# The tail of an eight-layer megakernel by pairs of sequences: last feed-forward layer, cross attention and second local stack in another order

## The chip, the core and the metric

The kernel runs on one core of a Trainium2 chip. The time is microseconds on the device for one launch; the profile is one execution taken by the hardware profiler. Five engines run side by side, each with its own instruction stream in a fixed order: TensorE (PE, with its weight loads shown apart as PEld), VectorE (DVE), ScalarE (ACT), GpSimd (POOL) and SyncE (SP, which here only issues DMAs). They wait for each other through semaphores.

## What is computed

The input `x` is eight sequences (B = 8) of 128 rows by 128 features; a context of 8 x 77 rows of 128 features stands beside it. Four blocks of layers follow each other, each of a cross attention and a feed-forward part. The change touches the end only, from the last of six layers of `L2_ffn` on. Cut to what matters, in float32:

```python
# L2_ffn: 6 layers, 16 heads of 64, window 32;  L3_ffn: 2 layers, 8 heads of 64, window 64
for i in range(DEPTH):
    x = attn_layer(shift_tokens(x), Wqkv[i], q_scale[i], k_scale[i], Wo[i]) + x
    x = ffn_layer(shift_tokens(x), ln_g[i], ln_b[i], W1[i], b1[i], W2[i], b2[i]) + x
# attn_layer: q, k normalised per head and rotated, softmax over a local window, times v, times Wo
# ffn_layer:  layer norm, a * gelu(gate) with 341 hidden features, times W2
x = x + L2_ffn(x)                                    # six layers inside, then the outer sum
x = x + L3_xattn(layernorm(x), context)              # 8 heads of 64 over 77 context rows
x = x + L3_ffn(layernorm(x))                         # two layers inside
```

Each sequence is independent of the others in these parts: sequence b of a layer needs only sequence b of the layer before. So the order in which sequences and layers are worked is free.

## The kernel before

All work is first recorded as steps in a plan, and then emitted. `Plan.add` takes the engines on which a step may run with an estimated duration, the values that it reads and writes and the buffers that it opens. The number of a step in this recording is its rank. `Plan.arranged` then runs a list scheduler over the steps: at each moment a free engine takes the ready step of lowest rank that is at most 600 ranks (for SP any number, unless `within` says otherwise) beyond the first step not yet started, and for whose buffers there is room. So the order of the calls in `plan_later` sets ranks, the scheduler sets the order on each engine, and this order is then fixed in the program. Buffers are shared by everything in this part: 48 of 128x512 floats ("big"), 8 banks of PSUM ("mm"), two rooms for attention weights ("w") and two for the rest of a layer's weights ("wr"). A step far ahead of the first unstarted one must leave a quarter of a kind free.

The pieces that the change orders, with their lines:

- `Local.first` (L1850) of one sequence and layer: `shifted` (L1900) transposes the sequences of a group, `projected` (L1911) makes queries and keys (matmuls of L1914), `queries_keys` (L1918) squares (L1935), rotates (L1936, L1938), sums (L1940) and adds (L1941) them, `inv_root` (L1960) makes the inverse norms, L1954 scales. `Blocks.turned` (L1785) then transposes through DRAM: DVE transposes blocks (L1793), SP writes them out (L1794) and reads them back (L1795).
- `Local.rest` (L1859) of one sequence: values, `weighed` (scores L2023, exponentials L2030), sums and outputs (`by_quarters` L2084, L2090 in L2_ffn, `by_halves` L2063, L2069 in L3_ffn), division (L2038 to L2052), projection (L1998) and the sum into `y` (L2002).
- `Local.gated` (L2099) of a group of sequences: shift (by DMA, L2114, in L2_ffn; by a matmul, L2120, in L3_ffn), layer norm, gates (L2145), gelu (L2152) with its loads of ACT's tables, L2159, L2161, down matmuls (L2169), and the sum into `y` or, at the last layer, `x` (L2174).
- `Local.end` (L1863) adds `y` to `x` (L1866, POOL); `Local.begin` (L1845) makes the layer norm of `x` for a group and starts a stack.
- `plan_xattn_64` (L1678): cross attention of four sequences (`half`): norm, one transposing step (L784), four query projections of 128x512 (L791), then `attend_64` (scores L970, softmax L834 to L853, outputs L981, projection L992) for one sequence after the other, and the sum into `x` (L1771). It yields between these pieces. Its keys and values were computed ahead of time and put into DRAM; `Kept.get` (L1759) loads them (L1761). An earlier block uses the same function with `kept=None`.
- `plan_later` (L2225): `order` is the list in which `first` and `rest` of all sequences are to be called. `some(n)` calls `first` for sequences a little ahead (two beyond the current one, in the second stack one), and then `rest` for the next. `along` steps through a cross attention between such calls.

Below, pair p is sequences 2p and 2p+1. In the tail the calls stand so: last layer of L2_ffn for pairs 0 and 1; `end` for both; cross attention of sequences 0 to 3 stepped through beside the last layer of pairs 2 and 3; `begin` of L3_ffn for sequences 0 to 3; `end` for 4 to 7; the second L3_ffn layer's weights; cross attention of sequences 4 to 7 beside the first L3_ffn layer of pairs 0 and 1; `begin` for 4 to 7; first layer of pair 2, attention of pair 0 in the second layer, first layer of pair 3, attention of pair 1; `gated` of the second layer for sequences 0 to 3 at once, and their store; then pairs 2 and 3.

Of the kernel before, what the change touches and what calls it, by code (L numbers as in the profile page):

```python
# [19 lines left out]
ALU = mybir.AluOpType  # L20
# [4 lines left out]
P = 128  # L25
B = 8
KC = 77
EPS = 1e-5
# [194 lines left out]
class Chip:  # L223
# [40 lines left out]
    def get(self, pack, name, lo=0, n=None):  # L264
        o, size = self.at[pack][name]
        return self.packs[pack][:, o + lo : o + (size if n is None else lo + n)]
# [56 lines left out]
def spread(ap, n, at):  # L323

    ap = ap.unsqueeze(at)
    shape = list(ap.shape)
    shape[at] = n
    return ap.to_broadcast(shape)
# [208 lines left out]
class Plan:  # L537
# [24 lines left out]
    def part(self, whole, get):  # L562

        return Val(None, lambda _: get(whole()), whole)
# [706 lines left out]
class Routed:  # L1271
# [251 lines left out]
    def behind(self, b, load):  # L1523

        self.w.c.tc.add_manual_dep(load.ins, self.got[b].name, mybir.DependencyInfo(
            mybir.DependencyClass.Sync, mybir.DependencyReason.DATA), reason="not in the way of these rows")
# [18 lines left out]
class Context:  # L1545
# [34 lines left out]
    def keys(self, h):  # L1580
        w = self.w
        c, nc = w.c, w.c.nc
        kT, kb, heads = w.tile([P, 4, KC]), self.kbs[h], c.get("cst", "heads4")
        self.rotated(kT, lambda: c.ctxT[:, h * 4 * KC : (h + 1) * 4 * KC], [], "k", 1, 4, KC)
        w.plan.add({"POOL": 2300}, lambda e: nc.gpsimd.tensor_tensor(
            kb().rearrange("p b i k -> p i b k"), spread(kT(), 4, 1), heads.unsqueeze(2).unsqueeze(3).to_broadcast([P, 4, 4, KC]),
            ALU.mult), [kT], [kb, *self.was[0]])
# [5 lines left out]
    def values(self, b):  # L1593
        c = self.w.c
        self.w.values_8(b, c.get("w", "L2_Wv"), c.get("row", "L2_xattn_bv"), self.vzs[b % 4])
# [82 lines left out]
def plan_xattn_64(w, nch, wq, wkv, wo, gamma, beta, bias, finish, kept=None):  # L1678


    c, nc, plan, inner = w.c, w.c.nc, w.plan, nch * P

    def half(h):
        xs = w.xs[4 * h : 4 * h + 4]
        xn, xT = w.tile([P, 4, P]), w.tile([P, 4, P])
        w.normed(lambda k: xn()[:, k, :], lambda k: xs[k](), xs, [xn], 1.0 + EPS, EPS * EPS)
        tp = w.turn(lambda k: xn()[:, k, :], [xn], opens=[xT])
        plan.add({"DVE": 683}, lambda e: nc.vector.tensor_scalar(xT(), tp(), gamma, beta, ALU.mult, ALU.add), [tp], [xT])
        for g in range(nch // 4):
            yield from group(h, g, xT)  # L1690

    def keys(h, k):
        ps, kT = w.bank([P, 4, KC]), w.tile([P, 4, KC])
        w.mm(lambda: ps().rearrange("p b k -> p (b k)"), lambda: wkv[:, k * P : (k + 1) * P],
             lambda: c.ctxT[:, h * 4 * KC : (h + 1) * 4 * KC], [], [ps], 520, opens=[kT])
        w.copy(kT, ps, [ps], [kT], 430, 470)
        return kT

    def values(b, g):
        ps, v = w.bank([KC, 512]), w.tile([KC, 512])  # L1700
        w.mm(ps, lambda: c.ctxT[:, b * KC : (b + 1) * KC], lambda: wkv[:, inner + g * 512 : inner + (g + 1) * 512], [], [ps],
             860, opens=[v])
        w.copy(v, ps, [ps], [v], 591, 682)
        return v

    def ahead():

        return [v for h in range(2) for v in (*(keys(h, k) for k in range(nch)), *(values(4 * h + j, 0) for j in range(4)))]

    def group(h, g, xT):  # L1710
        qTs = []
        if kept is None:
            kTs, v_of = [keys(h, k) for k in range(4 * g, 4 * g + 4)], lambda b: values(b, g)
        else:
            kTs = [kept.get([P, 4, KC], 8 * h + k) for k in range(4)]
            v_of = lambda b: kept.get([KC, 512], 8 * h + 4 + b % 4)
        for k in range(4 * g, 4 * g + 4):
            ps, qT = w.bank([P, 4 * P]), w.tile([P, 4 * P])
            w.mm(ps, lambda k=k: wq[:, k * P : (k + 1) * P], lambda: xT().rearrange("p b s -> p (b s)"), [xT], [ps], 860,
                 opens=[qT])  # L1720

            def part(e, qT=qT, ps=ps):
                if e == "ACT":
                    nc.scalar.mul(qT(), ps(), 0.125)
                else:
                    nc.vector.tensor_scalar(qT(), ps(), 0.125, None, ALU.mult)

            plan.add({"ACT": 597, "DVE": 683}, part, [ps], [qT])
            qTs.append(qT)
        yield  # L1730
        for j in range(4):
            b = 4 * h + j
            finish(b, w.attend_64(qTs, j * P, kTs, j, v_of(b), wo[:, 4 * g : 4 * g + 4, :],
                                  bias if g == 0 else None))
            if j < 3:
                yield

    return (half, ahead, kept) if kept else half


class Kept:
# [14 lines left out]
    def flat(t):  # L1756
        return t if len(t.shape) == 2 else t.rearrange("p b k -> p (b k)")

    def get(self, shape, i):  # L1759
        v = self.w.tile(shape)  # L1760
        self.w.plan.add({"SP": 500}, lambda e: self.w.c.nc.sync.dma_start(  # L1761
            self.flat(v()), self.rooms[i][: shape[0], 0 : int(np.prod(shape[1:]))]), [self.there[i]], [v], within=300)
        return v


# [456 lines left out]
    w.ys = [w.plan.fixed(w.y[:, b, :]) for b in range(B)]  # L2222


def plan_later(w, route, l2x, l2, l3x, l3, stored):  # L2225


    order = [(l2, l, b) for l in range(6) for b in range(B)]
    order += [(l3, l, b + j) for l, b in ((0, 0), (0, 2), (0, 4), (1, 0), (0, 6), (1, 2), (1, 4), (1, 6)) for j in range(2)]
    given = set()  # L2230
    at = {"first": 0, "rest": 0}

    def some(n):

        for i in range(n):
            while at["first"] < min(at["rest"] + 1 + (2 if at["rest"] < 48 else 1), len(order)) and order[at["first"]] in given:
                loc, l, b = order[at["first"]]
                loc.first(l, b)
                at["first"] += 1
            loc, l, b = order[at["rest"]]  # L2240
            loc.rest(l, b)
            at["rest"] += 1
            if i < n - 1:
                yield

    def side_by_side(*parts):
        for _ in zip_longest(*parts):
            pass

    def each(one, bs):  # L2250
        for b in bs:
            one(b)
            yield

    def begin(loc, b0, n):
        loc.begin(b0, n)
        given.update((loc, 0, b0 + k) for k in range(n))

    def gated(loc, l, b0, n=4):
        loc.gated(l, b0, n)  # L2260
        given.update((loc, l + 1, b0 + k) for k in range(n))

    def last(b0, n):
        l3.gated(1, b0, n, True)
        stored(b0, n)

    (one, layer), (l3x, ahead, kept) = l2x, l3x
    ahead = ahead()
    for k in range(4):
        side_by_side(each(one, (2 * k, 2 * k + 1)))  # L2270
        if k == 0:

            behind = lambda transfer: route.behind(1, transfer)
            kept.put(ahead, [w.xs[1]], behind)
            l2.layers[0] = l2.weights(0, [w.xs[1]], behind)
            w.plan.add({"SP": 5000}, lambda e: behind(w.c.load("w3")), [w.xs[1]], [])
        layer(2 * k, 2)
        begin(l2, 2 * k, 2)
    def along(steps, *counts):
        for n in counts:  # L2280
            side_by_side(some(1))
            for _ in range(n):
                next(steps, None)

    def pairs(loc, l, b0, n):
        for b in range(b0, b0 + n, 2):
            side_by_side(some(2))
            gated(loc, l, b, 2)

    side_by_side(some(4))  # L2290
    plan_flag(w)
    gated(l2, 0, 0, 2)
    gated(l2, 0, 2, 2)
    pairs(l2, 0, 4, 4)
    for l in range(1, 5):
        pairs(l2, l, 0, B)
    pairs(l2, 5, 0, 4)
    l2.end(0, 4)
    steps = l3x(0)
    along(steps, 0, 1)  # L2300
    gated(l2, 5, 4, 2)
    along(steps, 1, 1)
    gated(l2, 5, 6, 2)
    for _ in steps:
        pass
    begin(l3, 0, 4)
    l2.end(4, 4)
    l3.layers[1] = l3.weights(1)
    steps = l3x(1)
    for b in (0, 2):  # L2310
        along(steps, 1, 1)
        gated(l3, 0, b, 2)
    for _ in steps:
        pass
    begin(l3, 4, 4)
    for b in (4, 6):
        pairs(l3, 0, b, 2)
        side_by_side(some(2))
    last(0, 4)
    for b in (4, 6):  # L2320
        side_by_side(some(2))
        last(b, 2)


def store(c, out, b0, n):
# [83 lines left out]
```

## Time and profile before

| what | us |
|---|---|
| median of 3 runs (lowest, highest) | 1453.41 (1450.79, 1457.18) |
| the profiled execution, whole | 1462.85 |
| its span, first to last instruction | 1461.1 |
| TensorE busy in the span | 1343.9 |
| DVE, ACT, POOL busy in the span | 1111.7, 841.5, 837.9 |
| the stretch 1190 to 1461.1: TensorE busy | 228.7 of 271.1 |
| the same stretch: DVE, ACT, POOL busy | 185.5, 144.5, 125.2 |

Lines of the profile name the engine, the source line and the operation, then output tile <- input tiles, partitions x elements, and how many. A bracket at the end of a row of the timeline gives the idle time before it and what ended that. "PEclk" is the clock that TensorE was granted, as a share of full speed. One float32 matmul shows as two instructions, so "x6" of L2145 is three matmuls.

The last layer of L2_ffn runs from about 1120 to 1245 us, the cross attention of L3 between about 1190 and 1300, and L3_ffn from 1235 to the end. In the layers before (600 to 1100 us) TensorE is busy 475.9 of 500 us and DVE 466.2.

### The profile page before, as it was taken

The page shows a single profiled execution, that of the slowest core. Times are in us where ns is not written, and L with a number is a line of the kernel's source. Part 1 is how long each engine was busy: PE and PEld are TensorE (multiplying, and loading weights), DVE is VectorE, ACT ScalarE, POOL GpSimd, SP SyncE. Part 2 cuts the span into 40 slices and gives each one's busy share as a digit, 9 for nine tenths or more (in the row PEclk, how much of TensorE's full clock was granted, in tenths as well). Part 3 has the DMA queues.
Part 4 walks back from the last instruction along what each step waited for, and adds up shares of the span by engine and source line. Part 5 has one row for each costly group of instructions (what it writes and reads, how often), then busy time and mean ns, then how long its engine had stood idle before and what let it go on. Part 6 is the DMA issues. An engine that isn't in the chain of part 4 may idle for free. (4 is left out here: it accounts for less than half of the span.)

```text
span 1461.1 us, 39652 instructions
## 1 busy us (share of the span) xinstructions
PE 1343.9 (92%) x15451; PEld 949.1 (65%) x15451; DVE 1111.7 (76%) x2344; ACT 841.5 (58%) x1752; POOL 837.9 (57%) x1343
## 2 busy tenths in 40 slices
PE   8999999898888899999999999999899997798986
PEld 7777777665675566566666766766566766474655
DVE  7543676423478998998999989998889965869772
ACT  4565565243435457566666666766556754565653
POOL 4210236310577886876778767786768842738461
PEclk9999999999999999999999999999999999899998
DMA  9401001489421456455446545654654561304230
GB/s 309 167 1 44 2 2 59 132 300 354 141 70 37 138 182 209 154 176 193 151 143 223 180 127 170 201 165 150 218 165 125 160 216 50 117 1 145 88 109 25
DMA packets 217612, 204.40 MB, mean 140 GB/s; under 512 B 31646, under 2 KB 166366, under 8 KB 216264
## 3 DMA queue, kind: packets, MB, share of 16 engines
q1 hardware_dynamic: 211528, 196.54, 41.2%
q0 software_dynamic: 1536, 3.15, 0.7%
q8 instruction: 123, 2.02, 0.6%
q10 hardware_dynamic: 4352, 2.10, 0.5%
q14 instruction: 73, 0.60, 0.1%
HBM read 129.49 MB, written 70.68 MB: 137 GB/s over the span
## 5 line engine op out<-in xcount | busy, mean ns | idle before, releaser
L1941 POOL TENSOR_TENSOR big<-big,big 128x512 f32<-128x512 f32 x224 | 284.8, 1279 | 106.2 <-DVE big L1938 76.8
L1914 PE MATMUL mm<-wide,big 128*128 128x512 f32 x672 | 310.3, 603 | 6.3 <-DVE big L773 3.0
L771 ACT COPY big<-mm 128x512 f32<-128x512 f32 (+6 forms) x289 | 147.2, 519 | 162.3 <-PE mm L784 48.2
L1954 POOL TENSOR_TENSOR big<-big,few 128x512 f32<-128x512 f32 x224 | 227.3, 1045 | 1.9
L1935 ACT ACTIVATE big<-mm 128x512 f32<-128x512 f32 x224 | 132.4, 596 | 152.6 <-PE mm L1914 150.1
L1793 DVE STREAM_TRANSPOSE big<-big 128x512 f32<-128x512 f32 (+1 forms) x248 | 209.9, 867 | 10.8 <-POOL big L1954 10.2
L1914 PEld LDWEIGHTS mm<-wide,big 128*128 128x128 f32 x672 | 121.9, 192 | 133.4 <-issue 110.1
L1936 DVE TENSOR_TENSOR big<-mm,big 128x512 f32<-128x512 f32 x224 | 154.7, 691 | 15.1 <-ACT big L1935 13.4
L1938 DVE TENSOR_TENSOR big<-mm,big 128x512 f32<-128x512 f32 x224 | 153.9, 687 | 0.7 <-ACT big L1935 0.7
L1940 DVE TENSOR_REDUCE few<-big 128x8 f32<-128x512 f32 x224 | 152.4, 680 | 0.7 <-ACT big L1935 0.7
L2030 ACT ACTIVATE big<-mm 128x512 f32<-128x512 f32 x224 | 120.6, 600 | 50.7 <-PE mm L2023 48.2
L2023 PE MATMUL mm<-big,big 64*64 64x96 f32 (+2 forms) x3584 | 127.4, 275 | 7.2 <-DMA big<-blocks 4.7
L1998 PEld LDWEIGHTS mm<-narrow,big 128*128 128x128 f32 x896 | 108.5, 194 | 37.0 <-DVE big L2052 19.3
L2023 PEld LDWEIGHTS mm<-big,big 64*64 64x64 f32 x3584 | 125.8, 207 | 9.8 <-issue 5.6
L1998 PE MATMUL mm<-narrow,big 128*128 128x128 f32 x896 | 116.8, 282 | 16.5 <-DVE big L2052 8.9
L2090 PEld LDWEIGHTS mm<-big,big 128*32 128x32 f32 x3072 | 86.9, 110 | 28.1 <-issue 26.6
L784 PE MATMUL mm<-ident,big 128*128 128x128 f32 (+1 forms) x486 | 73.0, 284 | 33.0 <-ACT big L823 11.7
L2090 PE MATMUL mm<-big,big 128*32 128x128 f32 x3072 | 93.8, 273 | 0.0
L784 PEld LDWEIGHTS mm<-ident,big 128*128 128x128 f32 (+1 forms) x486 | 54.7, 144 | 59.4 <-ACT big L823 15.5
L773 DVE COPY big<-mm 77x512 f32<-77x512 f32 (+6 forms) x93 | 56.7, 624 | 46.3 <-PE mm L784 18.6
L2052 DVE SCALAR_TENSOR_TENSOR big<-mm,big 128x512 f32<-128x512 f32 x112 | 73.6, 684 | 2.0 <-PE mm L2090 0.3
L1495 DVE TENSOR_TENSOR big<-mm,p_col 128x512 f32<-128x512 f32 x32 | 20.7, 687 | 66.4 <-PE mm L784 55.6
(288 smaller groups left out, 2506.3 us busy)
## 6 DMA issues: line engine op xcount, KB each, us to landing
blocks<-big SPq DMA_DIRECT2D x224, 256.0 KB, 2.1
big<-blocks SPq DMA_DIRECT2D x224, 256.0 KB, 3.2
big<-in_experts_dram SPq DMA_DIRECT2D x128, 256.0 KB, 4.9
wide<-in_l2a_dram SPq DMA_DIRECT2D x6, 1536.0 KB
narrow<-in_l2b_dram SPq DMA_DIRECT2D x6, 534.0 KB, 10.9
narrow<-in_l2o_dram SPq DMA_DIRECT2D x6, 512.0 KB
blocks<-big SPq DMA_DIRECT2D x24, 128.0 KB, 1.9
big<-blocks SPq DMA_DIRECT2D x24, 128.0 KB, 3.4
```

Source lines behind the costliest of these rows:

```text
L771: nc.scalar.copy(out(), in_())
L1793: plan.add({"DVE": 150 + 138 * n}, lambda e: nc.vector.transpose(*within(u(), t())), [t], [u])
L1914: self.plan.add({"PE": 892}, lambda e: nc.tensor.matmul(ps(), lhsT=hs()[:, j, :], rhs=wqkv()[:, o : o + 512], start=True, stop=True), [hs, ...
L1935: yield lambda e: nc.scalar.activation(sq(), heads(), AF.Square)
L1936: yield lambda e: nc.vector.tensor_tensor(t1(), heads(), spread(rot()[:, 2 * kind, :], 8, 1), ALU.mult)
L1938: yield lambda e: nc.vector.tensor_tensor(halves(t2()), halves(heads())[:, :, ::-1, :], sin(), ALU.mult)
L1940: yield lambda e: nc.vector.tensor_reduce(ss()[:, lo : lo + 8], sq(), AX.X, ALU.add)
L1941: yield lambda e: nc.gpsimd.tensor_tensor(t1(), t1(), t2(), ALU.add)
L1954: plan.add({"POOL": 1062}, lambda e, t=t, t1=t1, i=i: nc.gpsimd.tensor_tensor(t().rearrange("p (c g d) -> p g c d", c=4, g=8), t1().rearra ...
L1998: nc.tensor.matmul(out(), lhsT=oT()[:, k, :], rhs=wo()[:, 4 * g + k, :], start=(g == 0 and k == 0), stop=(4 * g + k == nch - 1))
L2023: nc.tensor.matmul(sc[s]()[at : at + 64, k, q:end], lhsT=kT()[lo : lo + 64, k, at : at + 64], rhs=of_q(k, lo, q, end), start=False, stop=( ...
L2090: nc.tensor.matmul(avs[half]()[32 * t : 32 * t + 32, k, :], lhsT=vs[t // 2]()[:, at : at + 32], rhs=prs[t]()[:, k, :], start=True, stop=True)
```

## The change

The cross attention is made for any run of sequences (`part(b0, n)`) instead of halves, and the kept keys are loaded for two sequences (columns `b0 % 4 * KC` on of the kept tile, 154 of 308), so 16 loads of keys instead of 8. The estimates handed to the planner become formulas in n that give nearly the same numbers for n = 4. `LAST` writes out the order by pairs: A is the last layer of L2_ffn, X the cross attention, C and D the two layers of L3_ffn. Cross attentions that were begun are stepped through beside the following pieces, one step of each at a time; before C of a pair its cross attention is run to its end, and `begin` follows for the pair. `end` follows each A. The second layer's weights are no longer asked for early, but where that layer's first `first` stands. The look-ahead of `some` in L3_ffn goes from one sequence to two. D is done by pairs throughout, so its `gated` and the stores too: four of each instead of three.

```diff
@@ plan_xattn_64 @@
+    def part(b0, n, *parts):
+        xs = w.xs[b0 : b0 + n]
+        xn, xT = w.tile([P, n, P]), w.tile([P, n, P])
+        w.normed(lambda k: xn()[:, k, :], lambda k: xs[k](), xs, [xn], 1.0 + EPS, EPS * EPS, n=n)
+        tp = w.turn(lambda k: xn()[:, k, :], [xn], opens=[xT], n=n)
...
+        for at, m in parts or ((0, n),):
+            for g in range(nch // 4):
+                yield from group(b0 + at, m, g, lambda at=at, m=m: xT()[:, at : at + m, :], xT)
+
     def half(h):
...
+        return part(4 * h, 4)
...
-            kTs = [kept.get([P, 4, KC], 8 * h + k) for k in range(4)]
+            h = b0 // 4
+            kTs = [kept.get([P, n, KC], 8 * h + k, b0 % 4 * KC) for k in range(4)]
...
-            ps, qT = w.bank([P, 4 * P]), w.tile([P, 4 * P])
+            ps, qT = w.bank([P, n * P]), w.tile([P, n * P])
@@ plan_later @@
+LAST = "A0 A1 X0 A2 X1 A3 C0 X2 X3 C1 C2 C3 D0 D1 D2 D3".split()
...
-    order = [(l2, l, b) for l in range(6) for b in range(B)]
-    order += [(l3, l, b + j) for l, b in ((0, 0), (0, 2), (0, 4), (1, 0), (0, 6), (1, 2), (1, 4), (1, 6)) for j in range(2)]
+    order = [(l2, l, b) for l in range(5) for b in range(B)]
+    order += [({"A": l2, "C": l3, "D": l3}[k], {"A": 5, "C": 0, "D": 1}[k], 2 * int(p) + j) for k, p in LAST if k != "X" for j in range(2)]
...
-            while at["first"] < min(at["rest"] + 1 + (2 if at["rest"] < 48 else 1), len(order)) and order[at["first"]] in given:
+            while at["first"] < min(at["rest"] + 1 + (2 if at["rest"] < 48 else 2), len(order)) and order[at["first"]] in given:
...
-    pairs(l2, 5, 0, 4)
-    l2.end(0, 4)
-    steps = l3x(0)
-    along(steps, 0, 1)
-    gated(l2, 5, 4, 2)
-    along(steps, 1, 1)
-    gated(l2, 5, 6, 2)
-    for _ in steps:
-        pass
-    begin(l3, 0, 4)
-    l2.end(4, 4)
-    l3.layers[1] = l3.weights(1)
-    steps = l3x(1)
-    for b in (0, 2):
-        along(steps, 1, 1)
-        gated(l3, 0, b, 2)
-    for _ in steps:
-        pass
-    begin(l3, 4, 4)
-    for b in (4, 6):
-        pairs(l3, 0, b, 2)
-        side_by_side(some(2))
-    last(0, 4)
-    for b in (4, 6):
-        side_by_side(some(2))
-        last(b, 2)
+    attending = []
+
+    def along(steps):
+        for _ in steps:
+            for ahead in attending:
+                next(ahead, None)
+
+    for k, p in LAST:
+        b = 2 * int(p)
+        if k == "X":
+            attending.append(l3x(b, 2))
+            continue
+        if k == "C":
+            for _ in attending[0]:
+                pass
+            attending.pop(0)
+            begin(l3, b, 2)
+        along(some(2))
+        next_of = {"A": lambda: gated(l2, 5, b, 2), "C": lambda: gated(l3, 0, b, 2), "D": lambda: last(b, 2)}
+        next_of[k]()
+        if k == "A":
+            l2.end(b, 2)
```

On the engines, the programs are alike up to some place between 1120 and 1160 us of the profile before. After that TensorE's order puts pair 0's cross attention among the last L2_ffn layer of pairs 2 and 3, the projections of pair 0's first L3_ffn layer before the last feed-forward of pair 3, the cross attention of pairs 2 and 3 among the first L3_ffn layer of pairs 0 and 1, and all first layers ahead of nearly all second layers. From the scores of sequence 6 in the second layer on, the order is the same in both.

More of the change, by code (lines that the diff above doesn't have):

```diff
@@ L1681, in plan_xattn_64, with keys @@
     c, nc, plan, inner = w.c, w.c.nc, w.plan, nch * P
-    def half(h):
[L1684 to L1693, printed above, removed]
+    def part(b0, n, *parts):
[3 more added lines that the diff above has]
+        tp = w.turn(lambda k: xn()[:, k, :], [xn], opens=[xT], n=n)
+        plan.add({"DVE": 145 + 134 * n}, lambda e: nc.vector.tensor_scalar(xT(), tp(), gamma, beta, ALU.mult, ALU.add), [tp], [xT])
+        for at, m in parts or ((0, n),):
+            for g in range(nch // 4):
+                yield from group(b0 + at, m, g, lambda at=at, m=m: xT()[:, at : at + m, :], xT)
+    def half(h):
+        return part(4 * h, 4)
+    def keys(b0, n, k):
+        ps, kT = w.bank([P, n, KC]), w.tile([P, n, KC])
         w.mm(lambda: ps().rearrange("p b k -> p (b k)"), lambda: wkv[:, k * P : (k + 1) * P],
-             lambda: c.ctxT[:, h * 4 * KC : (h + 1) * 4 * KC], [], [ps], 520, opens=[kT])
-        w.copy(kT, ps, [ps], [kT], 430, 470)
+             lambda: c.ctxT[:, b0 * KC : (b0 + n) * KC], [], [ps], 130 * n, opens=[kT])
+        w.copy(kT, ps, [ps], [kT], 130 + 75 * n, 150 + 80 * n)
         return kT
@@ L1706, in ahead, with group, scale @@
     def ahead():
-        return [v for h in range(2) for v in (*(keys(h, k) for k in range(nch)), *(values(4 * h + j, 0) for j in range(4)))]
-    def group(h, g, xT):
+        return [v for h in range(2) for v in (*(keys(4 * h, 4, k) for k in range(nch)), *(values(4 * h + j, 0) for j in range(4)))]
+    def group(b0, n, g, of_x, xT):
         qTs = []
         if kept is None:
-            kTs, v_of = [keys(h, k) for k in range(4 * g, 4 * g + 4)], lambda b: values(b, g)
+            kTs, v_of = [keys(b0, n, k) for k in range(4 * g, 4 * g + 4)], lambda b: values(b, g)
         else:
-            kTs = [kept.get([P, 4, KC], 8 * h + k) for k in range(4)]
+            h = b0 // 4
+            kTs = [kept.get([P, n, KC], 8 * h + k, b0 % 4 * KC) for k in range(4)]
             v_of = lambda b: kept.get([KC, 512], 8 * h + 4 + b % 4)
         for k in range(4 * g, 4 * g + 4):
-            ps, qT = w.bank([P, 4 * P]), w.tile([P, 4 * P])
-            w.mm(ps, lambda k=k: wq[:, k * P : (k + 1) * P], lambda: xT().rearrange("p b s -> p (b s)"), [xT], [ps], 860,
+            ps, qT = w.bank([P, n * P]), w.tile([P, n * P])
+            w.mm(ps, lambda k=k: wq[:, k * P : (k + 1) * P], lambda: of_x().rearrange("p b s -> p (b s)"), [xT], [ps], 215 * n,
                  opens=[qT])
-            def part(e, qT=qT, ps=ps):
+            def scale(e, qT=qT, ps=ps):
                 if e == "ACT":
@@ L1726, in part @@
                     nc.vector.tensor_scalar(qT(), ps(), 0.125, None, ALU.mult)
-            plan.add({"ACT": 597, "DVE": 683}, part, [ps], [qT])
+            plan.add({"ACT": 180 + 104 * n, "DVE": 145 + 134 * n}, scale, [ps], [qT])
             qTs.append(qT)
         yield
-        for j in range(4):
-            b = 4 * h + j
+        for j in range(n):
+            b = b0 + j
             finish(b, w.attend_64(qTs, j * P, kTs, j, v_of(b), wo[:, 4 * g : 4 * g + 4, :],
                                   bias if g == 0 else None))
-            if j < 3:
+            if j < n - 1:
                 yield
-    return (half, ahead, kept) if kept else half
+    return (part, ahead, kept) if kept else half
 class Kept:
@@ L1757, in flat, with get @@
         return t if len(t.shape) == 2 else t.rearrange("p b k -> p (b k)")
-    def get(self, shape, i):
+    def get(self, shape, i, lo=0):
         v = self.w.tile(shape)
         self.w.plan.add({"SP": 500}, lambda e: self.w.c.nc.sync.dma_start(
-            self.flat(v()), self.rooms[i][: shape[0], 0 : int(np.prod(shape[1:]))]), [self.there[i]], [v], within=300)
+            self.flat(v()), self.rooms[i][: shape[0], lo : lo + int(np.prod(shape[1:]))]), [self.there[i]], [v], within=300)
         return v
@@ L2278, in plan_later @@
         begin(l2, 2 * k, 2)
[L2279 to L2283, printed above, removed]
     def pairs(loc, l, b0, n):
```

## The prediction

> **What bounds the kernel now.** I read the page's parts 1 and 2 first, then busy time by stretch over the tail, then TensorE's own instructions in order of time.
>
> ```profile
> span 1461.1 us, 39652 instructions
> PE 1343.9 (92%) x15451; PEld 949.1 (65%) x15451; DVE 1111.7 (76%) x2344; ACT 841.5 (58%) x1752; POOL 837.9 (57%) x1343
> ...
> PE   8999999898888899999999999999899997798986
> ...
> PEclk9999999999999999999999999999999999899998
> ```
>
> TensorE is busy 92% of the span, and its weak slices lie at the end, in the part that the change reorders. Stretches of that part (columns: busy us and count for PE, PEld, DVE, ACT, POOL; then granted clock, DMA share, GB/s):
>
> ```profile
> 1190.00:1226.00 36.00, 32.81 (x489) 26.21 (x478) 24.44 (x64) 20.15 (x56) 8.59 (x18) 1.00 0.34 115
> 1226.00:1266.00 40.00, 27.57 (x110) 15.10 (x110) 25.09 (x52) 17.58 (x36) 24.48 (x40) 0.79 0.26 84
> 1266.00:1306.00 40.00, 38.70 (x517) 30.83 (x514) 30.79 (x82) 26.65 (x68) 10.77 (x21) 1.00 0.17 55
> 1306.00:1350.00 44.00, 35.73 (x259) 20.85 (x257) 38.19 (x63) 25.68 (x55) 36.52 (x63) 0.92 0.36 115
> 1350.00:1388.00 38.00, 36.39 (x364) 24.37 (x362) 28.83 (x57) 23.08 (x47) 17.36 (x32) 1.00 0.28 90
> 1388.00:1424.00 36.00, 31.53 (x212) 19.49 (x216) 27.17 (x50) 20.36 (x39) 22.86 (x39) 0.91 0.34 110
> 1424.00:1461.10 37.10, 26.00 (x193) 19.91 (x192) 11.01 (x28) 11.04 (x21) 4.59 (x12) 0.81 0.09 24
> ```
>
> Full stretches alternate with weak ones. In the weak ones before the end the clock falls too, so idle time is paid twice:
>
> ```profile
> 1212.30 1.46 PE L2145 MATMUL mm<-big,narrow 128*128 128x256 f32 x6
> ...
> 1230.49 2.93 PE L2145 MATMUL mm<-big,narrow 128*128 128x256 f32 x6 [3.90 <-ACT big L2135]
> ...
> 1241.75 7.89 PE L1914 MATMUL mm<-wide,big 128*128 128x512 f32 x18
> 1256.69 1.63 PE L784 MATMUL mm<-ident,big 128*128 128x128 f32 x4 [7.05 <-ACT big L823]
> ```
>
> The same six gate matmuls (L2145) take 1.46 us warm and 2.93 us after the gap. From such rows, idle plus excess over the warm row, five stalls come out:
> - A, 1226 to 1238: idle 3.90 + 1.48, excess 1.47 + 1.15 (L2145, L2159): 8.0. The feed-forward of pair 3 in layer 5, then the norm of all four sequences 0 to 3, have nothing beside them.
> - B, 1250 to 1265: idle 7.05, excess 0.97 + 0.81 + 1.13 (L784, L2023, L791): 10.0. Four sequences' projections are issued, and the next cross attention waits for all of pairs 2 and 3.
> - C, 1307 to 1318: idle 1.37 + 0.54 + 0.64 + 1.48, excess 1.84: 5.9. The four-wide norm of sequences 4 to 7.
> - D, 1328 to 1348: idle 4.2, excess 1.8: 6.0. Scores wait for their block transposes.
> - E, 1388 to 1402: idle 4.1, excess 2.55: 6.6. Pair 3's first layer is late.
>
> Sum 36.5 us. The end from 1424 is a chain (scores, attention, shift, norm, gates, down, store).
>
> **The change, part by part.** *What is computed per sequence stays.* The eight 128x512 query matmuls become sixteen 128x256: TensorE time the same (L1914's 0.43 per instruction against L2145's 0.22). Their evictions: ACT's 128x256 copy is 354 ns against 598 for 128x512, so 16 x 0.354 - 8 x 0.598 = +0.9 us, on ACT and DVE, which were busy 144.5 and 185.5 of these 271 us. The roots of four-wide norms (POOL 0.19 + 1.03 + 0.25 + 0.20 = 1.67) become two two-wide ones (0.19 + 0.75 + 0.24 + 0.20 = 1.38): five of them, +5.4 us of POOL, busy 125 of 271. These lie beside TensorE: 0. Uncovered they would cost the 6.3.
>
> *The last feed-forward in pairs* adds a switch of ACT's tables. Row: L2154 loads take 1283 ns, with 0.1 us idle before six of them. The Trainium skill, "ScalarE: Activation LUTs", section "What ACT_TABLE_LOAD costs", speaks against it: about 1.28 us for the load plus 1.38 us of drain per switch. Two more loads: 2.6 us by the row, 5.3 by the page. I take the row, and nothing on the path, since pairs 0 and 1 of the last layer are followed by other sequences' work; uncovered 2.6.
>
> *Kept keys by pairs.* 16 key loads of 77 KB for 8 of 154 KB, values as before: 24 loads for 16.
>
> ```profile
> L1761 SPq DMA_DIRECT2D big<-kept x16: 297/424/522, 1155.0 to 1236.7; - x16
> ...
> DMA to landing us min/median/max: 4.6/5.0/5.4
> ```
>
> Eight issues more are 8 x 0.42 = 3.4 us of SP, in order with the block transfers (L1794, L1795). In the new order eleven kept loads stand among those of the last layer's sequences 3 to 7, and five between the transposed output and input of pair 3's gate; 5 x 0.42 = 2.1, against the 1.8 us which SP waited there for the output to land. Waits on a freed buffer are new there; behind such a load stand block inputs, and scores wait for these. SP's worst wait at L1761 was 0.5 us. Bounds: 0 and 8 x 0.5 + 3.4 = 7.4; I take 1.5, near the row.
>
> *The order* is the point. Durations below are sums of warm rows standing between two TensorE steps in the changed order ("cover"), against the chain outside TensorE.
> - A: pair 0's norm now follows cross attention of sequence 1. Chain: add 0.30, statistics 0.6, root 1.4 with gaps 0.3, scaling 0.9, handovers 1: 4.5; cover 2.5 (a transposing step 0.5, scores 0.65, pair 2's down matmuls 1.35): 2.0 left. Pair 3's gate chain took 18.2 us (last L1998 end 1212.3 to L2145 at 1230.5), cover 16 with the 2.0: 2.2 left. With clock about 5.0; saved 3.0.
> - B: projections to scores took 20.9 us for the first of four sequences (1237.74 to 1258.68); without the queue of four, rows add to 18.2 (projection 0.86, squares and reductions 4.9, root 2.7, scale 2.0, transposes 1.7, out 2.1, in 3.2, issues 0.8). Cover in the new order: four projections and two values 5.2, pair 3's gates and down 4.0, cross attention of sequences 2 and 3 4.6, queries and scores of the next 3.2: 17. Left 1.2 to 3.9; I take 2.5, with clock 4.0; saved 6.0.
> - C: the norms of pairs 1, 2, 3 have covers 4.5, 10 and 3.2 against 4.5: 1.3 left, and 1.3 from transpose to gates of pair 1: 2.6; saved 3.3.
> - D: covers of the first scores of pairs 1 and 2 are 18.2 and 18.3, left 0 to 2.8 each: 2.8 together; saved 3.2.
> - E: pair 3's first layer now stands ahead of the whole last layer; its shift has 6.4 of cover against 3.9 for shift to transpose (1442.72 to 1446.60), and the last layer's scores have 21 to 36. Left 0.6; saved 6.0.
> - The end: from the scores of sequence 6 on, TensorE's order is the same in both. Saved 0.
>
> Saved 21.5, less 1.5 for SP: **20 us**. Against the profiled execution, 1462.85, that gives 1443; the median of the runs shown is 1453.41, 9.4 lower, and the same subtraction gives **1433**. What is late next is DVE: work issued to it in the tail is nearly that of TensorE.
>
> The other rule: the Trainium skill, "TensorE: Matmul & The Clock Gate", "Part 1: The HAM clock gate (the "warmup" mystery)", has the clock halved after an idle window of about 3.4 us. Rows: C's gaps of 1.37, 0.54 and 0.64 in 2.6 us halved it as well (L2145 2.45, clock 0.83), and E's did. By the rule only A and B carry an excess, and the saving loses up to the 1.84 + 1.8 + 2.55 in C to E, 6.2: 14 us. I take the rows.
>
> **Rivals.**
> 1. *All five stalls go*: 1453.4 - 36.5 = 1417. For it: covers exceed those of before nearly everywhere. Against: A and B keep chains that are longer than their cover.
> 2. *The stalls move*: DVE sets the pace. For it: DVE ran 38.19 of 44 us from 1306 to 1350; cross attention's reductions now fall among the projections' DVE work. Against: 27 and 31 in the two full stretches. If A to D save a third of their 15.5 (5.2), E half of its 6.0 (3.0), and SP costs 4.0: gain 4.2, 1449.
> 3. *Slower: the pulled-forward cross attention starves the last layer.* From 1150 to 1190 TensorE has almost no slack (busy 38.95 of 40 us), and 48 big buffers are shared; two cross attentions in flight hold up to twenty (four keys, four queries, inputs, values each). A kept load that waits for a buffer holds SP, and all block inputs behind it. Sixteen such loads at 2.3 us each cost 37; less the 21.5: 1453 + 15 = 1469. It decides from 1.8 us a load on (29 against 21.5 + 7.3). For it: waits on TensorE appear ahead of those loads. Against: 0.5 us at worst before.
> 4. *The change doesn't do what it says*: the planner may undo the order. The emitted order shows it done, so I give it nothing.
>
> **How the numbers follow.** Forecast 0.53 (own range 1423 to 1445), all gone 0.21, moved 0.14, slower 0.12. What a measurement can tell from no change is 0.5%, 7.3 us: the first two are faster, 0.74; same 0.14; slower 0.12. The range takes in rival 1 and SP's upper bound and rival 2: 1415 to 1454.
>
> **What would show it.** Right: the tail's PEclk back near full, no TensorE gap over 4 us before the end, first scores of the second stack about 17 to 21 us after its first projection with cross attention between them; ACT with one more pair of table loads. Wrong: kept loads waiting over 2 us on SP, DVE at 10 of 10 us with TensorE idle, or new gaps in layer 5's last pairs.

## The result

| | us |
|---|---|
| before, median of 6 runs (lowest, highest) | 1455.3 (1450.79, 1465.59) |
| after, median of 6 runs | 1436.97 (1432.76, 1441.17) |
| ratio, 95% interval | 0.9845 [0.9819, 0.987] |
| profiled execution after (before: 1462.85) | 1436.21 |

The changed kernel is faster: the interval of the ratio stays clear of 1. The ratio of 0.9845 amounts to 22.6 us on 1455.3, while the two medians differ by 18.3. The forecast was 20 us less, 1433. Lines of code after the change have numbers higher by 5: L1914 is L1919, L1998 is L2003, L2023 is L2028, L2145 is L2150, L2169 is L2174.

The page of the changed kernel, parts 1 and 2:

```profile
span 1434.4 us, 39795 instructions
PE 1338.0 (93%) x15481; PEld 950.8 (66%) x15481; DVE 1109.2 (77%) x2350; ACT 850.7 (59%) x1775; POOL 842.3 (59%) x1367
...
PE   9999999898989899999999999999999999999996
...
PEclk9999999999989899999999999999999999999998
```

TensorE's weak slices of before, near the end, are gone but for the last one. Busy time by stretch of the changed kernel (columns as in the prediction):

```profile
1190.00:1210.00 20.00, 20.00 (x361) 17.34 (x350) 11.67 (x30) 11.50 (x29) 3.13 (x8) 1.00 0.28 83
1210.00:1242.00 32.00, 27.55 (x223) 20.67 (x225) 25.48 (x66) 20.44 (x47) 22.09 (x49) 0.89 0.26 79
1242.00:1290.00 48.00, 45.30 (x493) 32.07 (x484) 39.34 (x90) 35.28 (x92) 22.94 (x42) 1.00 0.22 69
1290.00:1304.00 14.00, 11.14 (x84) 8.65 (x84) 8.57 (x22) 9.86 (x22) 11.29 (x23) 1.00 0.32 105
1304.00:1350.00 46.00, 43.45 (x418) 26.90 (x417) 43.47 (x80) 29.58 (x62) 35.66 (x61) 1.00 0.50 164
1350.00:1397.60 47.60, 45.47 (x392) 30.64 (x390) 40.55 (x79) 32.57 (x62) 29.25 (x52) 1.00 0.33 105
1397.60:1434.40 36.80, 25.12 (x193) 18.79 (x192) 11.62 (x30) 10.98 (x21) 4.58 (x12) 0.88 0.09 26
```

Ahead of the end, one stretch has a lowered clock (0.89), where before there were three (0.79, 0.92, 0.91), and in none does TensorE idle more than 4.5 us. TensorE's instructions of the changed kernel in order of time, at the places of the old stalls:

```profile
1224.57 1.56 PE L2150 MATMUL mm<-big,narrow 128*128 128x256 f32 x6
...
1229.59 0.66 PE L784 MATMUL mm<-ident,big 128*77 128x128 f32 x4 [1.13 <-DVE big L853]
...
1233.86 2.93 PE L2174 MATMUL mm<-narrow,big 128*128 128x128 f32 x12
...
1242.44 1.11 PE L2028 MATMUL mm<-big,big 64*64 64x128 f32 x32
...
1300.04 0.33 PE L784 MATMUL mm<-ident,y_res 128*128 128x128 f32 x1 [1.99 <-ACT y_res L823]
```

Pair 3's gates (1224.57) and the second stack's first scores (1242.44) come without a gap; before, they stood behind 3.90 and, with the cross attention, 7.05 us. The longest gap ahead of the end is 1.99 us, at the norm of one pair.

**A yardstick for all runs.** The down matmuls of pair 0 in layer 5 (from 1152.99 before, 1151.54 after) are a landmark of every kernel, just where the orders begin to part. The time from the matmul that follows them to the end is called the *tail* here; what differs from chip to chip or from one execution to the next ahead of the landmark stays out of it. The tail before, and after:

```profile
1154.33:1461.10 306.77, 263.34 (x2622) 180.43 (x2620) 214.08 (x450) 168.52 (x365) 150.75 (x261) 0.93 0.30 98
1152.88:1434.40 281.52, 254.32 (x2652) 180.46 (x2650) 212.25 (x456) 177.91 (x388) 157.09 (x291) 0.97 0.33 105
```

So the tail fell by 25.3 us: TensorE's idle time by 16.2 (43.4 to 27.2), its busy time by 9.0.

### The profile page after: what moved, and what is told of

Same layout as the page of the kernel before. It is cut to its first block, busy times and chain, and to the rows that moved or that the text cites. A ratio compares the mean times of both kernels' runs of the same rounds, so it can differ in the third digit from the quotient of the medians.

```text
span 1434.4 us, 39795 instructions
## 1 busy us (share of the span) xinstructions
PE 1338.0 (93%) x15481; PEld 950.8 (66%) x15481; DVE 1109.2 (77%) x2350; ACT 850.7 (59%) x1775; POOL 842.3 (59%) x1367
## 5 line engine op out<-in xcount | busy, mean ns | idle before, releaser
L1919 PE MATMUL mm<-wide,big 128*128 128x512 f32 x672 | 310.8, 601 | 2.3 <-DVE y_res L2007 1.2
L771 ACT COPY big<-mm 128x512 f32<-128x512 f32 (+6 forms) x298 | 150.9, 517 | 157.0 <-PE mm L784 45.9
L1919 PEld LDWEIGHTS mm<-wide,big 128*128 128x128 f32 x672 | 120.9, 191 | 124.3 <-issue 107.3
L2003 PEld LDWEIGHTS mm<-narrow,big 128*128 128x128 f32 x896 | 108.9, 194 | 41.8 <-DVE big L2057 20.9
L2003 PE MATMUL mm<-narrow,big 128*128 128x128 f32 x896 | 116.8, 282 | 18.8 <-DVE big L2057 11.1
L2028 PEld LDWEIGHTS mm<-big,big 64*64 64x64 f32 x3584 | 124.9, 207 | 2.6 <-issue 1.9
L2028 PE MATMUL mm<-big,big 64*64 64x64 f32 (+2 forms) x3584 | 125.4, 274 | 1.2 <-DMA big<-blocks 1.1
L773 DVE COPY big<-mm 77x512 f32<-77x512 f32 (+5 forms) x89 | 52.5, 603 | 31.2 <-PE mm L1253 12.0
```

The costliest lines, as they stand in the source:

```text
L771: nc.scalar.copy(out(), in_())
L1919: self.plan.add({"PE": 892}, lambda e: nc.tensor.matmul(ps(), lhsT=hs()[:, j, :], rhs=wqkv()[:, o : o + 512], start=True, stop=True), [hs, ...
L2003: nc.tensor.matmul(out(), lhsT=oT()[:, k, :], rhs=wo()[:, 4 * g + k, :], start=(g == 0 and k == 0), stop=(4 * g + k == nch - 1))
L2028: nc.tensor.matmul(sc[s]()[at : at + 64, k, q:end], lhsT=kT()[lo : lo + 64, k, at : at + 64], rhs=of_q(k, lo, q, end), start=False, stop=( ...
```

## The experiments

The experiments ran on three chips, on which the kernel before took 1472.83, 1459.45 and 1473.57 us; so ratios to before on the same chip stand here, with their intervals, and tails from one profile each. A tail's difference from 306.8 departs from what the ratio gives by up to 4 us, so smaller differences between tails say little.

| kernel | ratio | tail | TensorE idle in it |
|---|---|---|---|
| before | 1 | 306.8 | 43.4 |
| after | 0.9845 [0.9819, 0.987] | 281.5 | 27.2 |
| late_second | 1.0016 [0.9997, 1.0035] | 305.2 | 48.4 |
| d0_early | 0.9917 [0.989, 0.9944] | 293.2 | 37.6 |
| begin4b | 0.9952 [0.9937, 0.9967] | 296.4 | 38.7 |
| x_fours | 0.9964 [0.9945, 0.9983] | 297.7 | 41.7 |
| begin4_d0 | 0.994 [0.9918, 0.9962] | 297.1 | 38.2 |
| c0_early | 0.9991 [0.9976, 1.0006] | 306.1 | 45.0 |
| shared_keys | 0.9874 [0.9849, 0.9899] | 287.6 | 32.2 |
| after_ahead1 | 0.9844 [0.9818, 0.987] | 283.8 | 30.8 |
| before_ahead2 | 1.0034 [1.0016, 1.0052] | 311.5 | 51.0 |
| before_warm | 0.9974 [0.9962, 0.9987] | 303.0 | filled with dummies |
| after_warm | 0.9845 [0.9821, 0.9869] | 284.4 | filled with dummies |
| single_end | 0.9802 [0.9776, 0.9829] | 277.9 | 25.7 |

### One part alone: second layers last

The kernel before, with the second layers behind all first layers, as in the changed kernel, and by pairs (`late_second`):

```diff
-((0, 0), (0, 2), (0, 4), (1, 0), (0, 6), (1, 2), (1, 4), (1, 6))
+((0, 0), (0, 2), (0, 4), (0, 6), (1, 0), (1, 2), (1, 4), (1, 6))
...
-        side_by_side(some(2))
-    last(0, 4)
-    for b in (4, 6):
+    for b in (0, 2, 4, 6):
```

> The kernel before with one part of the change: all first layers of L3_ffn ahead of the second layers, and the second layer's end by pairs; cross attention, norms and look-ahead as before. My theory (each stall goes by its own cover): only stall E goes, 6.0 us, so about 1449 us, ratio 0.996. Rival (the order of the last two layers is what brings the gain, the cross attention by pairs little): 1436 to 1440, ratio 0.988 or less. TensorE gaps near 1226, 1250 and 1307 us stay by my theory.

Nothing came of it. Stall E did go. The stretch of this kernel, and that of the kernel before in its place:

```profile
1363.00:1417.00 54.00, 52.00 (x545) 38.41 (x540) 41.34 (x85) 37.32 (x71) 28.40 (x53) 1.00 0.34 104
1348.00:1402.00 54.00, 48.67 (x446) 32.97 (x438) 39.55 (x82) 30.53 (x61) 30.57 (x56) 0.94 0.31 101
```

But TensorE idles elsewhere instead, in the whole tail 5.0 us more than before. TensorE of this kernel in order of time:

```profile
1360.06 1.55 PE L2023 MATMUL mm<-big,big 64*64 64x128 f32 x28 [3.88 <-DMA big<-blocks]
...
1459.69 0.86 PE L784 MATMUL mm<-ident,big 128*128 128x128 f32 x2 [3.41 <-ACT big L823]
```

The stretch around the first gap, in the same kernel:

```profile
1336.50:1363.00 26.50, 19.90 (x147) 10.92 (x147) 26.50 (x43) 14.25 (x31) 24.85 (x39) 0.94 0.47 153
```

DVE is busy for all of 26.5 us there. In this place of the kernel before (stall D, 1316.56 to 1348) it was nearly as full, 30.58 of 31.44 us, so its load alone does not tell the two apart. Its order does in part: here six rotations (L1936) stand ahead of DVE's first block transpose (L1793), which starts 12.3 us after the first projections of the stretch, where before it was four and 9.3 us. In the end the gap ahead of the transposes is 3.41 us, where before it was 1.56. So a stall that is covered alone moves; this is what rival 2 had described.

### One part taken back, three times

Pair 0's second layer goes ahead of pair 3's first one (`d0_early`):

```diff
-C0 X2 X3 C1 C2 C3 D0 D1 D2 D3
+C0 X2 X3 C1 C2 D0 C3 D1 D2 D3
```

> The changed kernel with pair 0's second layer put back between the first layers of pairs 2 and 3, everything else as changed. My theory: stall E comes back, +6, about 1443 us, ratio 0.991. Rival (the order of the last layers brings most): about 1452, ratio 0.998. Rival (it brings nothing): 1437, ratio 0.9845.

`begin` for four sequences at once, behind both their cross attentions (`begin4b`):

```diff
-            for _ in attending[0]:
-                pass
-            attending.pop(0)
-            begin(l3, b, 2)
+            if b % 4 == 0:
+                for _ in range(2):
+                    for _ in attending.pop(0):
+                        pass
+                begin(l3, b, 4)
```

> The changed kernel, but the second stack begins for four sequences at once, as before: the first layer of pair 0 waits for the cross attention of pairs 0 and 1, that of pair 2 for pairs 2 and 3; cross attention itself still by pairs. My theory: A, B and C come back in part (their saved 3.0 + 6.0 + 3.3), +8 to +12, 1445 to 1449 us, ratio 0.993 to 0.996, with TensorE idle over 4 us between the first projections of L3_ffn and its first scores. Rival (the early start of the cross attention does it, not the pairwise begin): 1437 to 1439.

Cross attention of four sequences at a time, `begin` by pairs (`x_fours`):

```diff
-LAST = "A0 A1 X0 A2 X1 A3 C0 X2 X3 C1 ...
+LAST = "A0 A1 X0 A2 A3 C0 X2 C1 ...
...
-            attending.append(l3x(b, 2))
+            attending.append(l3x(b, 4))
...
-            for _ in attending[0]:
-                pass
-            attending.pop(0)
+            if b % 4 == 0:
+                for _ in attending.pop(0):
+                    pass
```

> The changed kernel with the cross attention of four sequences at a time (one norm, four-wide queries, eight key loads), begun after pairs 1 and 3 of layer 5 as before; begin by pairs and the rest of the order stay. If the prediction's stall B comes from cross attention waiting for all of pairs 2 and 3, 6 us or more come back: 0.989 to 0.992. If the pairwise begin alone removes A to C, nothing comes back: 0.9845 within 0.002.

The first two ratios came out as expected, 0.9917 and 0.9952. The third lost more than expected, 0.9964 instead of 0.989 to 0.992. Where the time comes back is seen in TensorE's instructions, first with the second layer of pair 0 early:

```profile
1413.03 1.13 PE L2003 MATMUL mm<-narrow,big 128*128 128x128 f32 x8 [3.09 <-DVE big L2057]
...
1420.44 1.98 PE L2028 MATMUL mm<-big,big 64*64 64x128 f32 x32 [3.64 <-DMA big<-blocks]
...
1439.92 1.16 PE L2003 MATMUL mm<-narrow,big 128*128 128x128 f32 x8 [2.77 <-DVE big L2057]
...
1445.33 0.86 PE L784 MATMUL mm<-ident,big 128*128 128x128 f32 x2 [3.38 <-ACT big L823]
```

These four gaps hold 12.9 us, for a tail 11.6 us longer than that of the changed kernel. But they are not stall E in its old place: from 1360 us up to them TensorE's clock is full and no gap is over 1 us. It is the end that grew, to 49.8 us where the changed kernel needs 36.80 for nearly the same number of matmuls (192 and 193):

```profile
1360.00:1410.50 50.50, 46.08 (x390) 30.49 (x387) 37.25 (x73) 30.12 (x58) 21.29 (x38) 1.00 0.28 89
1410.50:1460.30 49.80, 28.27 (x192) 20.52 (x192) 16.42 (x35) 13.86 (x25) 11.29 (x24) 0.72 0.16 50
```

So the size was forecast right and the place was not. With `begin` for four:

```profile
1247.08 1.14 PE L784 MATMUL mm<-ident,big 128*77 128x128 f32 x4 [2.67 <-POOL big L853]
...
1273.99 1.98 PE L2028 MATMUL mm<-big,big 64*64 64x128 f32 x32 [3.54 <-DMA big<-blocks]
...
1318.99 1.10 PE L784 MATMUL mm<-ident,y_res 128*128 128x128 f32 x3 [1.75 <-ACT y_res L823]
...
1347.88 1.27 PE L2028 MATMUL mm<-big,big 64*64 64x128 f32 x32 [1.86 <-DMA big<-blocks]
```

Softmax and block inputs (A and B), the norm (C) and scores (D) have gaps again, those of A to C smaller than before. From the first projections of L3_ffn (1253.64) to its first scores TensorE idles 4.6 us, over 4 as expected. With cross attention by fours:

```profile
1256.59 0.41 PE L2022 MATMUL mm<-band_L_ffn,identb 64*64 64x512 bf16 x4
1265.64 1.98 PE L2028 MATMUL mm<-big,big 64*64 64x128 f32 x32 [8.64 <-DMA big<-blocks]
...
1331.74 0.86 PE L784 MATMUL mm<-ident,y_res 128*128 128x128 f32 x2 [6.55 <-ACT y_res L823]
```

TensorE has nothing between the band masks and the first scores for 8.64 us: stall B as it was (7.05). The second gap is the norm that `begin` makes, waiting behind a four-wide cross attention: C, 6.55 us where before it was four gaps of 4.0 together. The two make 15.2 of the 16.2 us that the tail is longer.

Against a total of 25.3 us of tail the three take back 11.6, 14.9 and 16.2, together 42.7. By the ratios they take back 0.7, 1.1 and 1.2%, together 3.0 of a gain of 1.55%. So the parts need each other: each one taken back takes with it some of what the others had gained.

### Two parts taken back at once

The edits of the early second layer and of `begin` for four together (`begin4_d0`).

> The changed kernel with both edits at once that cost it time singly: begin for four sequences (0.9952 alone) and the second layer of pair 0 ahead of the first layer of pair 3 (0.9917 alone), the changed kernel being at 0.9845. If these two carry separate stalls and hold all of the gain between them, the losses add: 0.9845 + 0.0107 + 0.0072 = 1.0024, about the kernel before. If they meet in the same stall, or if cross attention by pairs carries a part of its own, it stays lower: 0.993 to 0.998.

0.994, the same as `begin` for four alone (0.9952) within the intervals: not 1.0024. With one batch left in the order, the other one costs nothing more. The 0.6% that remain belong to the rest of the change; which part of it wasn't tried.

### The suspected costs

Key loads for four sequences, each used by two pairs (`shared_keys`: 8 loads as before, and keys held longer):

```diff
-            kTs = [kept.get([P, n, KC], 8 * h + k, b0 % 4 * KC) for k in range(4)]
+            if b0 % 4 == 0:
+                whole[h] = [kept.get([P, 4, KC], 8 * h + k) for k in range(4)]
+            kTs, off = whole[h], b0 % 4
...
```

> The changed kernel with the kept keys loaded for four sequences at once and used by two pairs: 8 loads of 154 KB as before instead of 16 of 77 KB, held longer. My theory put 1.5 us on the extra loads in SP's queue: 1435.5 us, the same within what can be measured. Rival (kept loads hold SP's queue and starve the last layer): 7 us or more faster, 1430. If buffers held longer matter more: slower than 1437.

Fewer loads gain nothing; 0.9874 lies, if anything, on the slower side. Since the keys are held longer as well, this run does not price the loads alone. The queue shows little waiting. Kept loads (L1766) of the changed kernel, their durations in ns, the time to landing, and SP's longest wait for a buffer there (in total, times, longest):

```profile
L1766 SPq DMA_DIRECT2D big<-kept x24: 289/423/543, 1122.2 to 1271.9; - x24
...
DMA to landing us min/median/max: 1.9/2.3/3.8
```

```profile
SPq L1766 <- ACT big L2046: 1.4, 1, 1.4
```

The look-ahead, put back to 1 in the changed kernel (`after_ahead1`, shown), and put to 2 in the one before (`before_ahead2`):

```diff
-(2 if at["rest"] < 48 else 2)
+(2 if at["rest"] < 48 else 1)
```

> The changed kernel with the look-ahead in L3_ffn put back to one sequence. My theory counts cover from the order as emitted and gives the look-ahead no price of its own: about 1438 us, within 4 of the changed kernel. Rival (the wider look-ahead feeds TensorE and brings a good part): 1443 or more.

> The kernel before with nothing changed but the look-ahead in L3_ffn, two sequences instead of one. My theory: A and C stay, since nothing is ready to run beside the four-wide norms: 1453 us, ratio 0.995 to 1.002. Rival (look-ahead brings a good part): 1448 or less, ratio 0.995 or less.

Nothing in the one (0.9844), and 0.3% slower in the other (1.0034, where at most 1.002 was expected). The look-ahead is no part of the gain.

### The clock apart from the order

The planner can put matmuls whose result nobody reads into places where it expects TensorE to idle; its time limit for that was 60 us, and is lifted (`before_warm`, `after_warm`):

```diff
-with work(c, "later", BUFS_C, False, 60.0) as w:
+with work(c, "later", BUFS_C, False, 10000.0) as w:
```

> The kernel before; where the planner sees TensorE idle for 0.4 us in this part, it now puts a dummy matmul of 128x128 (it did so in the first 60 us only; 221 more stand in the program). Nothing of the computation changes. If idle time is paid twice through the clock, the excess over the warm rows that I counted (2.6, 2.9, 1.8, 1.8, 2.6 in A to E, some 6 at the end) falls by a third to a half: 1447 to 1451 us, granted clock over 0.985 instead of 0.978. Rival (the clock's part is small, or dummies stand in the way of work that comes sooner than planned): 1455 or more.

> The changed kernel with the same dummies (139 more). What is left of the clock's part, some 3 us in the middle and some 5 at the end, may halve: 1433 us, the fastest so far. Rival: no change or slower, 1437 to 1442, since dummies delay real matmuls.

In the kernel before, the clock of the whole tail rises to full, and 0.26% is gained, about what was expected:

```profile
1150.55:1453.50 302.95, 287.81 (x3006) 212.98 (x3004) 208.36 (x444) 169.43 (x369) 149.86 (x261) 1.00 0.31 99
```

In the changed kernel the mean clock of the whole execution rises from 0.985 to 0.993, and the time stays, where a gain was expected. The dummies (L733) stand ahead of real work at times. In the end of the kernel before with dummies, DVE has the last inputs ready at 1443.12, and the matmuls that need them start 3 us later, behind 34 dummies:

```profile
1441.78 1.34 DVE L2161 SCALAR_TENSOR_TENSOR big<-mm,p_col,big 128x256 f32<-128x256 f32 x3 [2.16 <-ACT big L2152]
...
1442.37 3.96 PE L733 MATMUL mm<-ident,ones 128*128 128x128 f32 x34
1446.17 1.50 PE L2169 MATMUL mm<-narrow,big 128*128 128x128 f32 x12
```

So these runs give the net of a full clock and of delays, and not what a full clock is worth.

### A better version?

The first L3_ffn layer of pair 0 ahead of the last L2_ffn layer of pair 3 (`c0_early`):

```diff
-A0 A1 X0 A2 X1 A3 C0 X2 X3
+A0 A1 X0 A2 X1 C0 A3 X2 X3
```

> The changed kernel with the first L3_ffn layer of pair 0 ahead of the last L2_ffn layer of pair 3 (order A0 A1 X0 A2 X1 C0 A3 X2 X3 C1 C2 ...). If what is left in the changed kernel's 1210 to 1242 (4.5 us idle and some 2.5 us of half clock) comes from too little work beside pair 3's chains, it gains 2 to 4 us: 0.982. If the work that it takes from 1242 to 1304 is missed there, the stalls only move: 0.9845 to 0.989.

All of the gain but 0.1% is lost, more than either forecast had it; TensorE idles 17.8 us more than in the changed kernel. At its largest gap:

```profile
1277.36 0.44 PE L784 MATMUL mm<-ident,y_res 128*128 128x128 f32 x2
1283.85 1.10 PE L784 MATMUL mm<-ident,big 128*77 128x128 f32 x4 [6.04 <-DVE big L853]
```

Softmax of the later cross attentions (L853) stands bare here. That pair 0's layer, pulled forward, is the work missing beside it fits the order, but this gap is only a third of the added idle time, and the rest wasn't traced.

And the last pair of the last layer, one sequence after the other (`single_end`):

```diff
+        if k + p == "D3":
+            for j in range(2):
+                along(some(1))
+                last(6 + j, 1)
+            continue
```

> The changed kernel with the last pair of the second layer handled one sequence after the other (feed-forward, end and store of sequence 6 before the attention output of sequence 7). The last 36.8 us hold 11.7 us of TensorE idle. If the chain's length goes by the width of its instructions, the end shrinks by 2 to 4 us: 0.982. If it goes by the number of steps and ACT's table loads (2 x 1.28 us more), it grows by 1 to 4 us: 0.985 to 0.988.

0.9802 [0.9776, 0.9829], against 0.9845 [0.9819, 0.987] of the changed kernel on another chip: the intervals overlap a little, so the stretch itself is the better witness. From the scores of sequence 6 on, in this kernel:

```profile
1410.35:1442.30 31.95, 21.56 (x207) 17.20 (x206) 12.27 (x35) 11.43 (x25) 5.91 (x18) 0.96 0.11 30
```

31.95 us against 36.80, with the clock at 0.96 instead of 0.88. The tail ahead of it is 1.2 us longer, so 3.6 us remain, within the scatter of tails; the ratio points the same way. TensorE in this end:

```profile
1422.59 0.33 PE L2125 MATMUL mm<-y_res,p_cst 128*128 128x64 f32 x2
...
1426.09 1.05 PE L2003 MATMUL mm<-narrow,big 128*128 128x128 f32 x8
...
1429.69 0.83 PE L2150 MATMUL mm<-row,narrow 128*128 128x128 f32 x6
...
1432.21 0.93 PE L2150 MATMUL mm<-row,narrow 128*128 128x128 f32 x6 [0.50 <-DVE row L2144]
```

The shift of sequence 6 (1422.59) now comes before the projection of sequence 7 (1426.09), its gates (1429.69) before those of sequence 7 (1432.21), and the chain left at the end is one sequence wide. The feared table loads did not come: there is one of 1283 ns in either end, since the gelus still follow each other without an exponential between.

## Why the prediction was right, and where it was not

- **A and B** (saved 9.0 in the forecast). Before: 18.0. After, 1210 to 1242: idle 4.45, and an excess of 3.4 in four cold groups (L2174 2.93 for 1.50, L981 1.98 for 1.09, L992 1.65 and 1.60 for 1.1). Saved 10.2. The gap forecast at pair 3's gate (2.2) isn't there, nor is B's 2.5: projections to scores took 23.6 us (1218.84 to 1242.44), longer than the 17 to 21 forecast, but TensorE was idle for 1.9 of it only.
- **C and D** (saved 6.5). Before: 11.9. After, 1290 to 1350: idle 5.4 at full clock. Saved 6.5. C's largest rest is 1.99 instead of 1.3; D's scores have no gap of a microsecond.
- **E** (saved 6.0). Before: 6.6. After, 1350 to 1397.6: idle 2.1. Saved 4.5 in the whole kernel. But "E: saved 6.0" was put to one step, the order of the second layers: that step alone gave 1.0016, and taking a part of it back cost 11.6 us of tail, in the end of the kernel and not at E.
- **The end** (0): 37.2 before, 36.8 after.
- **Not forecast:** 3.2 us. Before, 1190 to 1226 had 3.19 us of idle that were counted as nothing; after, 1190 to 1210 has none, since pair 0's cross attention lies there.
- **SP** (1.5 lost): no loss seen. The longest wait for a buffer was 1.4 us, loads landed after 2.3. Rival 3, slower from 1.8 us a load on, is refuted.
- **ACT's tables** (nothing on the path): two more pairs of loads in the program where one was forecast (22 for 20 ahead of the gelus, 30 for 28 behind, 1283 ns each). The sums leave no loss for them.

The sum, 10.2 + 6.5 + 4.5 + 0.4 + 3.2 = 24.8, is close to the tail's 25.3, closer than one profile each can warrant. The idle time that it leaves out, 1.3 and 1.6 us before (1266 to 1306, 1350 to 1388) and 2.7 after (1242 to 1290), cancels. In the nearness of 20 us there is some luck: the 3.2 and the 1.5 of SP were missed in one direction, E in the other, and the forecast lies between 18.3 (medians), 22.6 (ratio) and 25.3 (tail).

For the whole change, then, size and reasons were nearly right. What failed is the pricing of its parts: "Sum 36.5" and "saved 21.5" treat five stalls as five separate accounts, and the expectations for single parts were made so. The runs show one account. One part alone was worth nothing, and each of three parts taken back cost 46 to 64% of the tail's gain. That filling one hole takes work from beside another chain is how the gaps read; which work is missing where was traced in a few places only.

The second weak term is "idle time is paid twice". TensorE's busy time did fall by 9.0 us. By the rule of the Trainium skill ("TensorE: Matmul & The Clock Gate", Part 1), which halves the clock after an idle window of about 3.4 us, only A and B would carry an excess (5.5 us, of which 3.4 are still there), and it could have fallen by 2.1; the rows were the better guide to the clock. Yet filling idle time with dummies gained 3.8 us of tail (306.8 to 303.0) against 11.7 us of excess in A to E and some 6 in the end. Either slow matmuls, inside a stretch that waits for DVE or a DMA, mostly use up time that would else be idle, or the dummies' delays ate the gain: both fit, and the 3 us of delay in the end show that the second is part of it. The forecast needed no correction for it, since it removed the stalls themselves.

Rival 1, all gone, fell short by what is left: of the 36.5 us some 15 (7.8 in A and B, 5.4 in C and D, 2.1 in E). Rival 2's mechanism is real, but weak in the full change: DVE is busy 43.47 of 46 us from 1304 to 1350, and so is TensorE (43.45). One of the prediction's own signs of being wrong, DVE full with TensorE idle, shows twice, from 1320 to 1330 (1.45 us idle) and from 1370 to 1380 (10.00 and 9.07):

```profile
1320.00:1330.00 10.00, 8.55 (x81) 4.70 (x81) 10.00 (x17) 6.45 (x15) 9.34 (x15) 1.00 0.43 136
```

## What to carry to other kernels

When several stages in a row wait for a batch, change all of them to the smaller batch together before judging one: halfway versions move the stall, and the one part of the order tried alone here (1.0016) would have spoken against the whole. For each piece that is moved to fill a gap, check what stood beside it at its old place. When the middle is full, look at the last chain: nothing covers it, so make it narrow.

## What was not expected of the hardware

The clock fell to nearly half in the changed kernel after small gaps only. Stretches of it:

```profile
1226.00:1230.00 4.00, 2.87 (x27) 2.12 (x25) 4.00 (x9) 3.95 (x7) 3.75 (x7) 1.00 0.00 0
1230.00:1234.00 4.00, 3.87 (x28) 3.08 (x26) 3.97 (x11) 0.09 (x2) 3.05 (x7) 0.61 0.17 66
1234.00:1238.00 4.00, 4.00 (x20) 4.00 (x21) 0.70 (x2) 1.67 (x5) 1.58 (x5) 0.54 0.74 237
...
1298.00:1302.00 4.00, 1.85 (x15) 1.61 (x15) 1.66 (x4) 2.77 (x7) 2.80 (x9) 1.00 0.61 200
```

TensorE was busy 4.00 of 4 us at a granted 0.54, and the longest gap in the 24 us before 1230 was 1.13 us (five gaps, 3.7 us together). A gap of 1.99 us just before 1300, on the other hand, left the clock at 1.00. What tells the two apart wasn't tried.
